# Narrower third slot group and five VectorE steps handed to ScalarE in a four-layer graph network

## The chip, the cores and the metric

The kernel runs on one core of one Trainium2 chip, as one launch. The metric is the device time of that launch in microseconds (us), the median of three runs. Names used below: PE is TensorE (PEld its weight loads), DVE is VectorE, ACT is ScalarE, POOL is GpSimd, SP is SyncE, which here issues the DMAs.

## The reference

128 graphs of 64 nodes with 128 features each pass through four residual layers. An entry of `adj` is nonzero for about a quarter of the node pairs; it is both the edge mask and the edge weight. What matters here, cut from the reference:

```python
# layer 0: continuous filter over edges; h = relu(layernorm(x))
g  = exp(coeff * (e[..., None] - offsets)**2)            # 64 offsets per edge
Wf = ssp(g @ W1.T + b1) @ W2.T + b2                      # per edge, 128 wide
y  = einsum('bjf,bijf->bif', h @ Wa.T, Wf * A * A)
x  = x + ssp(y @ Wd1.T + bd1) @ Wd2.T + bd2              # ssp = softplus - ln 2
# layer 1: hyperbolic graph attention (c = 1)
res   = tanh(|mx| / |x| * artanh(|x|)) * mx / |mx|       # mobius_matvec, per node
h     = proj(mobius_add(proj(res), bias))
x_loc = 2 / lambda(h_i) * artanh(|s|) * s / |s|,  s = mobius_add(-h_i, h_j)   # per edge
att   = sigmoid(silu([x_self, x_loc] @ att_w1.T + att_b1) @ att_w2.T)
x     = x + (sum_j att * x_loc * mask -> MLP -> expmap, logmap, silu, expmap)
# layer 2: degree-normalised aggregation, layer 3: mean of messages and update
```

The artanh of a small argument divided by the argument is 1 + z/3 + z^2/5 + ..., z being the square of the argument.

## The kernel before

**Groups and pairs.** The graphs are worked off in 16 groups of 8. Two graphs lie side by side on the 128 partitions, so a group is 4 pairs (`NP`). Tiles named "dense" are 128 by 4 by 64, that is 256 columns: one entry per pair of nodes. Tiles named "tiny" are 128 by 4: one scalar per node. "Wide" tiles are 128 by 4 by 128.

**Slots.** The edge stages (`layer0`, `layer1_edges`) don't work on 64 by 64 dense entries. `order` sorts the nodes of each graph by degree, and each node gets slots for its neighbours: 8 in the first part, 8 more in the second, and a third part gives further slots to the nodes of the highest degrees alone. `BLOCKS` tells the three parts: in an entry `(k, r0, n, k0)`, `n` nodes from rank `r0` on get `k` slots each, for the neighbours from number `k0` on. The first two parts are one block and 512 columns wide, the third is six blocks and 264 columns. `spread` (a coefficient on each slot), `gather` (the sum over a node's slots) and the building of the one-hot tile `oh` at the end of `order` issue one DVE instruction per block. The other edge steps (filter matmuls on PE, exponentials, logarithms, Silu and Tanh on ACT, products on DVE) issue instructions as wide as the part. In the profile's shapes a form of 264 or 528 (twice 264) columns belongs to the third part, one of 512 or 1024 to the first two. At the very end `enough` compares every node's degree with what `BLOCKS` holds, by `STEPS`; where it doesn't suffice, a branch runs `dense_stack`, the same network over all 64 by 64 entries, after the slot version.

**Order of the work.** The program is straight-line code. `Weave` decides, when the program is built, in which order the steps of all stages are put on the engines: each stage is a generator that yields an engine whenever it goes on to another one, and the weave takes the step that can start first by the estimated durations in `about`; among steps about as early, the one with the lowest key. The key is the stage's due time (`2 * g` and an offset by stage) plus an entry of the table `LATE`, which lists corrections step by step. On the chip each engine then works off its own list in that order, and semaphores hold it where an input isn't ready. The functions Exp and Ln need one ACT table and Silu and Tanh another; the outer loop sets where the table is changed, four times a group.

**The steps that the change touches.**

- `layer1_nodes`, start: PE multiplies layer 0's sums by `wd1T` into a PSUM bank (`sm`); DVE adds the bias `bd1` into `spn` (tile `a0`, in the profile `a<-sm,c_L_gnn_bd`); DVE limits it, ACT takes Exp and Ln.
- `layer1_nodes`, node scalars: `s` is the limited norm; ACT takes two logarithms (`at_p`, `at_m`); DVE forms the artanh quotient `r`, then `z = s * s`, and `series` replaces `r` where `z` is small by a polynomial in `z` (tiles `at_z`, `at_m`).
- `layer1_nodes`, dense coefficients: the same with the dense tiles `rt` (the quotient), `e3` (shown as `e`) and `rs` (the polynomial).
- `layer1_nodes`, end: the dense coefficient `pq` (in tile `rs`) is split into three bf16 parts `pqs`: cast, subtract, cast, subtract, all on DVE.
- `layer1_edges`, `rows`: PE spreads `pqs` to the slots by `oh`; `rest1` and `rest2` are the node-wise end of layer 1 and layers 2 and 3 of an earlier group, woven between.

Of the kernel before, what the change touches and what calls it, by code (L numbers as in the profile page):

```python
# [11 lines left out]
F32 = mybir.dt.float32  # L12
U32 = mybir.dt.uint32
I32 = mybir.dt.int32
AF = mybir.ActivationFunctionType
ALU = mybir.AluOpType
AX = mybir.AxisListType

B, N, D = 128, 64, 128
NG = 64  # L20
NP = 4
GROUPS = B // (2 * NP)
P = 128
# [24 lines left out]
def dense_stack(ctx: ExitStack, tc: tile.TileContext, ins, out: bass.AP):  # L48
# [691 lines left out]
    with tc.manual_schedule(engines={mybir.EngineType.Activation}):  # L740
# [3 lines left out]
        for g in range(GROUPS):  # L744
# [11 lines left out]


BLOCKS = [[(8, 0, 64, 0)], [(8, 0, 64, 8)],
          [(20, 0, 1, 16), (13, 1, 4, 16), (8, 5, 8, 16), (6, 13, 7, 16), (4, 20, 15, 16),
           (2, 35, 13, 16)]]  # L760
WIDTHS = [sum(k * n for k, _, n, _ in c) for c in BLOCKS]
OFFS = [sum(WIDTHS[:i]) for i in range(len(WIDTHS))]
SLOTS = sum(WIDTHS)
RC = max(r + n for _, r, n, _ in BLOCKS[2])
STEPS = [(48, 2.0), (35, 2.0), (20, 2.0), (13, 2.0), (5, 5.0), (1, 7.0)]
SOFT_MAX = 40.0
LN2_HALF = float(0.5 * np.log(2.0))
ROOT_HALF = float(np.sqrt(0.5))
M_MAX = 40.0
# [2 lines left out]
PE, DVE, ACT, POOL = "PE", "DVE", "ACT", "POOL"  # L772
# [12 lines left out]
def about(engine, op, args, kw):  # L785
# [14 lines left out]
    if engine == ACT:  # L800
# [5 lines left out]


LATE = {
    "attention": (0, -0.5),
    "coefs_of": (1.25, 0.75, -2.25),  # L810
    "coefs_of2": (2.75,),
    "duo": (2.5, 3.5),
    "duo2": (0, 2.5, -2),
    "filter_of": (0.75, 3, -0.25, -2.25, -2, -2.75),
    "filter_of2": (-2.75, 1.75, 2.5, 1.75, -2.5),
    "layer1_nodes": (0, -0.25, 0, 0, 0, 0, 0, 3, -3.5, 0, 0, 0, -0.5, -5.5, 0, 2.25, -1.75, 0, 0, 0,
        0, 0, 0, -2.5, 0, 0, 0, 0, 0, -1.25, 0, 0, 0, 2, 0, 0.75, 0, 0, 0, 0, 0, 0, 0, 0, 0.5),
    "neighbours": (-0.25, -3.5),
    "neighbours2": (1.25,),
    "normed_x": (0, 0, 0, 0, 0, 0, 1.5),  # L820
    "one_minus_z": (3.75,),
    "order": (-0.25, -2.75, 2.25, 0, 0, -5, 0, -3.75, 0, 1.75, -6.75, -3, 3.5, 0, 0, -2.75, -2.75,
        3.25, 1.75, 0.5),
    "rest1": (-3, 0, 0, -3, 0, 0, 0, -3.5, -1.75, 0, 0, 0, 0, 0, -1.75, 0, 0, 0, 3.75),
    "rest2": (2.25, 4.5, 0, 0, 0, 0, 0, 0, 0, 0, 0, -4, 0, -3.75, 0, 1.25, 0, 0, 0, 0, -3, 0, -2.25,
        0, -3.5, 0, 0, 1.25, 3),
    "rows": (0, -1.25),
    "rows2": (2.5,),
    "scores_of": (-1.25, -1.5, -3.5, -1.5),
    "scores_of2": (0, -3.25, 0, -3.5),  # L830
    "slots_ranks": (3.5, 0, 4.75),
    "squares": (2.25, 9.5),
    "squares2": (0, 2.75),
    "turned_from": (3.5,),
    "weights_of": (-3,),
    "weights_of2": (0, -2.5, -2.25),
}


# [30 lines left out]
def on(engine, *takes, after=(), table=None):  # L870

    return engine, takes, after, table
# [98 lines left out]
def sparse_stack(ctx: ExitStack, tc: tile.TileContext, ins, out: bass.AP, flag):  # L971
# [3 lines left out]
    const = ctx.enter_context(tc.tile_pool(name="s_const", bufs=1))  # L975
    pers = ctx.enter_context(tc.tile_pool(name="s_pers", bufs=2))
    wide = ctx.enter_context(tc.tile_pool(name="s_wide", bufs=1))
    edge = ctx.enter_context(tc.tile_pool(name="s_edge", bufs=2))
    dense = ctx.enter_context(tc.tile_pool(name="s_dense", bufs=1))
# [4 lines left out]
    w = Weave()  # L984
    V, S, G, T = (Timed(e, name, w) for e, name in ((nc.vector, DVE), (nc.scalar, ACT),
                                                    (nc.gpsimd, POOL), (nc.tensor, PE)))
    BF, U16 = mybir.dt.bfloat16, mybir.dt.uint16

    def bl(ap, n):

        return ap.unsqueeze(len(ap.shape)).to_broadcast([*ap.shape, n])
# [19 lines left out]
    for e in (0.5, -0.5, -0.25):  # L1011
        exps[e] = const.tile([P, 2 * NP], F32, name=f"exp{len(exps)}")
        G.memset(exps[e], e)

    gi = const.tile([P, 1], I32, name="gi")
    G.iota(gi[0:NG, :], [[0, 1]], base=0, channel_multiplier=1)
# [34 lines left out]
    def column(name):  # L1051
        t = const.tile([P, 1], F32, name="c_" + name)
        nc.sync.dma_start(out=t, in_=ins[name].rearrange("(d o) -> d o", o=1))
        return t
# [31 lines left out]
    b1, bd1, b2s = (column("L0_gnn_" + n) for n in ("b1", "bd1", "b2"))  # L1086
# [130 lines left out]
    def wtile(name, bufs=None):  # L1217
        return wide.tile([P, NP, D], F32, name=name, tag=name, **({"bufs": bufs} if bufs else {}))

    def etile(name, bufs=1):  # L1220
        return dense.tile([P, NP, N], F32, name=name, tag=name, bufs=bufs)

    def ttile(name, *shape, bufs=1):
        return tiny.tile([P, *(shape or (NP,))], F32, name=name, tag=name, bufs=bufs)

    def flat(t):
        return t.rearrange("q p n -> q (p n)")
# [10 lines left out]
    act = S.activation  # L1238
# [30 lines left out]
    def reduce_d(dst, src):  # L1269
        V.tensor_reduce(dst, src, AX.X, ALU.add)  # L1270
# [36 lines left out]
    def normed(dst, x, mv, r):  # L1307

        V.tensor_tensor(dst, x, bl(mv[:, :, 0], D), ALU.subtract)
        V.scalar_tensor_tensor(dst, dst, 0.0, bl(r, D), ALU.max, ALU.mult)  # L1310

    def series(r, z, mask, poly):

        V.tensor_scalar(poly, z, 1.0 / 7, None, ALU.mult)
        for c in (1.0 / 5, 1.0 / 3):
            V.scalar_tensor_tensor(poly, poly, c, z, ALU.add, ALU.mult)
        V.tensor_scalar(poly, poly, 1.0, None, ALU.add)
        V.tensor_scalar(mask, z, 0.01, None, ALU.is_lt)
        V.copy_predicated(r, mask.bitcast(U32), poly)

    def root(dst, src, e):
# [4 lines left out]
    def artanh_over(r, s, hn):  # L1326
# [6 lines left out]
        V.tensor_scalar(E.bitcast(I32), E.bitcast(I32), 0x7F800000, None, ALU.bitwise_and)  # L1333
        V.tensor_scalar(ef, E.bitcast(I32), -float(127 << 23), LN2_HALF / (1 << 23),
                        ALU.add, ALU.mult)
# [38 lines left out]

    def slot_tile(name, c, prs, bufs=2):
        W, n = WIDTHS[c], prs.stop - prs.start
        t = edge.tile([P, NP * WIDTHS[2]], F32, name=name, tag=name, bufs=bufs)
        return t[:, 0:n * W].rearrange("q (p w) -> q p w", w=W)

    def prior(*keys):  # L1380
# [112 lines left out]
    def enough():  # L1493
# [3 lines left out]
        V.tensor_scalar(cap, deg, -16.0, None, ALU.add)  # L1497
        for r, more in STEPS:
            V.tensor_scalar(step, place, float(r), more, ALU.is_lt, ALU.mult)
# [154 lines left out]
    def layer1_nodes(g, st):  # L1654
# [4 lines left out]
        spn, ex = wtile("a0"), wtile("a1")  # L1659
        pt = bank()  # L1660
        pre = flat(pt)
# [2 lines left out]
        T.matmul(pre.rearrange("q (x r) -> q x r", r=N)[:, :, 0:RC], lhsT=wd1T, rhs=ys[2],  # L1664
                 start=False, stop=True)
        w.release("ys", st["ys_used"])
        yield on(DVE)
        V.tensor_scalar(flat(spn), pre, bd1, None, ALU.add)
        w.release("sm")
        V.tensor_scalar(ex, spn, SOFT_MAX, None, ALU.min)  # L1670
        w.event("soft_ready", g)
        yield on(ACT, table="log")
# [62 lines left out]
        s, r = ttile("s"), ttile("r")  # L1735
        V.tensor_scalar(s, xn, ATMAX, None, ALU.min)
        yield on(ACT, table="log")
        lp, lm = ttile("at_p"), ttile("at_m")
        act(lp, s, AF.Ln, bias=1.0, scale=1.0)
        act(lm, s, AF.Ln, bias=1.0, scale=-1.0)  # L1740
        yield on(DVE)
        z, rs, mask = ttile("at_z"), ttile("at_r"), ttile("at_k")
        V.tensor_tensor(lp, lp, lm, ALU.subtract)
        V.reciprocal(rs, s)
        V.scalar_tensor_tensor(r, lp, 0.5, rs, ALU.mult, ALU.mult)
        V.tensor_tensor(z, s, s, ALU.mult)
        series(r, z, mask, lm)
        arg = ttile("arg")
        V.tensor_tensor(arg, r, s, ALU.mult)
        V.tensor_tensor(arg, arg, rr[:, 0], ALU.mult)  # L1750
# [2 lines left out]
        te, t, tq = (ttile(f"th{k}") for k in range(3))  # L1753
# [93 lines left out]
        e1, e2, e3, e4, bR = (etile(n) for n in ("e1", "e2", "e3", "e4", "bR"))  # L1847
# [9 lines left out]
        rt, rs, mask = etile("rt"), etile("rs"), etile("mask")  # L1857
# [18 lines left out]
        V.tensor_scalar(rt, rt, ATMAX, None, ALU.min)  # L1876
        yield on(ACT, table="log")
        act(rt, rt, AF.Ln, bias=1.0)
        yield on(DVE, after=[("e4", g)])
        w.event("nodes_log", g)  # L1880
        V.scalar_tensor_tensor(rt, e4, -0.5, rt, ALU.mult, ALU.add)
        V.tensor_tensor(rt, rt, rs, ALU.mult)
        yield on(DVE)
        series(rt, e3, mask, rs)
        yield on(DVE)
        V.tensor_tensor(rt, rt, e2, ALU.mult)
        qd = dense.tile([P, NP, 2, N], F32, name="qd", tag="qd", bufs=2)
        qn, dc, mp, pq = qd[:, :, 0, :], qd[:, :, 1, :], etile("mp", 2), rs
# [6 lines left out]
        cs = ttile("cs", bufs=2)  # L1895
        reduce_d(cs, dc)

        yield on(DVE, after=[("U", g)])
        pqs = dense.tile([P, 3, NP, N], BF, name="pqs", tag="pqs")
        V.tensor_copy(pqs[:, 0], pq)  # L1900
        V.tensor_tensor(e4, pq, pqs[:, 0], ALU.subtract)
        V.tensor_copy(pqs[:, 1], e4)
        V.tensor_tensor(pqs[:, 2], e4, pqs[:, 1], ALU.subtract)

        yield on(DVE)
        Sx, S3 = st["Sx"], [wide.tile([P, NP, P], BF, name=f"Sx{k}", tag=f"Sx{k}") for k in range(3)]
        scaled(Sx, Sx, cs)
        for k in range(2):
# [360 lines left out]
def gnn_stack_kernel(tc: tile.TileContext, ins, out: bass.AP):  # L2269
    nc = tc.nc  # L2270
    with tc.tile_pool(name="flags", bufs=1) as flags:
        flag = flags.tile([P, 1], I32, name="flag")
        sparse_stack(tc, ins, out, flag)
        short = nc.values_load(flag[0:1, 0:1], min_val=0, max_val=P)
        with tc.If(short > 0):
            dense_stack(tc, ins, out)
# [26 lines left out]
```

## Time and profile before

| what | value |
|---|---|
| median of three runs | 2122.32 us (2122.26 to 2126.36) |
| the profiled execution: time, span | 2121.52 us, 2119.6 us |
| busy: PE, DVE, ACT, POOL | 1806.3, 1847.9, 1641.1, 364.5 us |
| mean granted TensorE clock | 0.94 |
| table loads on ACT | 64, 1283 ns each |
| DMA | 13.94 MB, 7 GB/s on average |

Busy time is the time in which an engine had an instruction in work. The profile names groups of instructions by the tile they write and the tiles they read, with the buffer numbers left out, then shape and type, count, total busy time and the mean duration of one. All instructions carry line 853, since a helper (`Timed`) issues them; so the tile names tell the steps apart. Durations of neighbouring DVE or ACT instructions overlap by some 0.07 to 0.1 us, so the distance from start to start is a little shorter than a duration where the second doesn't need the first's result, and a little longer where it does.

### The profile page before, as it was taken

What the parts mean: (1) busy time and instruction counts of PE and PEld (TensorE: products, weight loads), DVE (VectorE), ACT (ScalarE), POOL (GpSimd) and SP (SyncE); (2) the same over time, 40 slices, a digit from 0 to 9 for tenths busy, and PEclk for the clock granted to TensorE, in tenths of its full rate; (3) what the DMA queues carried; (4) which work ended last, traced back from release to release, by engine and by line L of the source; (5) the groups of instructions that cost most, each with busy time, mean ns of one, the idle gap of its engine ahead of it and who ended that gap; (6) DMA issues with size and microseconds to landing.
All of it is one profiled execution on the core that took longest, in us unless ns stands there. A gap on an engine that the chain in (4) does not pass through costs nothing.

```text
span 2119.6 us, 31941 instructions
## 1 busy us (share of the span) xinstructions
PE 1806.3 (85%) x11223; PEld 866.0 (41%) x11223; DVE 1847.9 (87%) x4828; ACT 1641.1 (77%) x3364; POOL 364.5 (17%) x362
## 2 busy tenths in 40 slices
PE   4869897998989898998989889898989889896773
PEld 2333343444444344444444444444434444443342
DVE  5669789999999999999999999999999999897742
ACT  3767887979698887979798897969888796975531
POOL 1011012021212203021221202121220302111121
PEclk9979999999999999999999999999999999997765
DMA  2000000000000000000000000000000000000000
GB/s 55 3 6 1 1 6 1 6 8 6 1 8 6 8 6 8 6 8 6 1 8 6 9 6 9 6 1 8 6 9 1 9 1 6 1 1 6 6 5 8
DMA packets 29531, 13.94 MB, mean 7 GB/s; under 512 B 10544, under 2 KB 29360, under 8 KB 29360
## 3 DMA queue, kind: packets, MB, share of 16 engines
q1 hardware_dynamic: 29360, 11.80, 2.1%
q8 instruction: 90, 1.47, 0.3%
q14 instruction: 81, 0.66, 0.1%
HBM read 7.61 MB, written 4.19 MB: 6 GB/s over the span
## 4 chain that ended last, share of the span: by engine, by line
PE 37%; DVE 36%; ACT 19%; issue 7%; POOL 0%; SPq 0%; DMA 0%; DVEq 0%; ACTq 0%; POOLq 0%
PE big L853 25%; PE sm L853 9%; ACT ex L853 6%; DVE va L853 5%; DVE ex L853 4%; PE sl L853 4%; ACT e L853 4%; DVE th L853 4%; DVE y L853 2%; ACT ra L853 2%; DVE ah L853 2%; DVE v L853 2%; ACT n L853 2%; DVE att L853 2%; DVE oh L853 1%
## 5 line engine op out<-in xcount | busy, mean ns | idle before, releaser
L853 PE MATMUL big<-ex,w2T 128*128 128x512 f32 (+1 forms) x768 | 320.2, 542 | 41.8 <-ACT ex L853 20.6
L853 ACT ACTIVATE ex<-big,c_L_gnn_att_b 128x1024 f32<-128x1024 f32 (+1 forms) x192 | 185.5, 974 | 105.0 <-PE big L853 103.2
L853 PE MATMUL big<-e,w1T 64*128 64x512 f32 (+1 forms) x768 | 201.5, 624 | 68.0 <-ACT e L853 47.8
L853 ACT ACTIVATE ex<-big,c_L_gnn_b 128x1024 f32<-128x1024 f32 (+1 forms) x192 | 185.7, 976 | 44.1 <-PE big L853 44.0
L853 PEld LDWEIGHTS big<-ex,w2T 128*128 128x128 f32 x768 | 131.7, 189 | 198.6 <-ACT ex L853 69.5
L853 PE MATMUL big<-va,U 64*128 64x512 f32 (+1 forms) x768 | 186.5, 563 | 29.1 <-DVE va L853 26.8
L853 PE MATMUL big<-va,a 64*128 64x512 f32 (+1 forms) x768 | 181.1, 568 | 10.7 <-DVE k_s L853 3.8
L853 PE MATMUL sl<-ex,aw2b 128*64 128x512 f32 (+1 forms) x768 | 180.7, 549 | 5.5 <-ACT th L853 4.3
L853 DVE SCALAR_TENSOR_TENSOR ex<-big,c_L_gnn_b,ra 128x1024 f32<-128x1024 f32 x128 | 163.7, 1279 | 16.0 <-PE big L853 15.6
L853 ACT ACTIVATE ex<-ex 128x1024 f32<-128x1024 f32 (+1 forms) x192 | 173.9, 925 | 0.2
L853 ACT ACTIVATE ra<-big 128x528 f32<-128x528 f32 (+1 forms) x192 | 166.3, 886 | 8.1 <-PE big L853 7.6
L853 DVE TENSOR_REDUCE y<-ex 128x128 f32<-128x1024 f32 x128 | 155.3, 1213 | 0.6
L853 ACT ACTIVATE th<-sl,hab 128x512 f32<-128x512 f32 (+1 forms) x192 | 118.1, 615 | 45.4 <-PE sl L853 45.4
L853 PE MATMUL big<-slot_r,Sx 64*128 64x512 bf16 (+1 forms) x1152 | 138.9, 346 | 0.0
L853 POOL TENSOR_TENSOR k_r<-k_r,exp 128x4 f32<-128x4 f32 x32 | 32.4, 1013 | 583.1 <-DVE k_r L853 578.7
L853 PEld LDWEIGHTS big<-e,w1T 64*128 64x128 f32 x768 | 68.9, 204 | 155.6 <-ACT e L853 55.1
L853 ACT ACTIVATE va<-va,sr 128x512 f32<-128x512 f32 (+1 forms) x192 | 123.1, 650 | 3.1 <-DVE va L853 2.9
L853 PE MATMUL big<-oh,pqs 64*64 64x512 bf16 (+1 forms) x1152 | 123.3, 348 | 0.0
L853 DVE COPY_PREDICATED va<-slot_r,big 128x1024 f32<-128x1024 uint16 (+1 forms) x96 | 106.5, 1111 | 9.7 <-PE big L853 9.7
L853 DVE SCALAR_TENSOR_TENSOR th<-th,oh 128x1024 f32<-128x1024 f32 (+1 forms) x80 | 99.2, 1240 | 13.8 <-ACT th L853 13.8
L853 ACT ACTIVATE e<-e 128x1024 f32<-128x1024 f32 (+2 forms) x144 | 106.7, 752 | 1.1
L853 PE MATMUL big<-va,ones 64*64 64x512 f32 (+1 forms) x768 | 97.4, 559 | 11.0 <-DVE va L853 11.0
(479 smaller groups left out, 3832.4 us busy)
## 6 DMA issues: line engine op xcount, KB each, us to landing
x<-in_x_dram SPq DMA_DIRECT2D x16, 256.0 KB, 2.9
out_dram<-v SPq DMA_DIRECT2D x16, 256.0 KB, 2.3
adj<-in_adj_dram SPq DMA_DIRECT2D x16, 128.0 KB, 2.3
rt<-in_L_gnn_att_w_dram SPq DMA_DIRECT2D x2, 64.0 KB, 1.9
rs<-in_L_gnn_mlp_w_dram SPq DMA_DIRECT2D x2, 64.0 KB, 2.0
wupd<-in_L_gnn_W_upd_dram SPq DMA_DIRECT2D x1, 128.0 KB, 3.6
w<-in_L_gnn_W_msg_dram SPq DMA_DIRECT2D x2, 64.0 KB, 3.3
r_L_gnn_bd<-in_L_gnn_bd_dram SPq DMA_DIRECT2D x1, 64.0 KB, 3.1
```

What stands on the lines that cost most here:

```text
L853: return f(*args, **kw)
```

## The change

The third part becomes five blocks with 242 columns in all (`STEPS` follows). The bias `bd1` is added by an ACT Identity. The two casts of `pqs` become ACT Copies. The polynomial of the small arguments becomes a square with a constant: 0.2 z^2 + z/3 + 1 = (A z + B)^2 + (1 - B^2), with the square on ACT, in a tile of its own (`poly` for the dense, `at_r` for the tiny one), and the constant added on DVE; the bound below which it is used goes from 0.01 to 0.006. The tiny `z` itself becomes an ACT Square. The table `LATE` has new entries, so the order of the instructions on every engine is another one. The slot tiles shrink from 1056 to 1024 columns.

```diff
 BLOCKS = [[(8, 0, 64, 0)], [(8, 0, 64, 8)],
-          [(20, 0, 1, 16), (13, 1, 4, 16), (8, 5, 8, 16), (6, 13, 7, 16), (4, 20, 15, 16),
-           (2, 35, 13, 16)]]
+          [(18, 0, 2, 16), (11, 2, 4, 16), (7, 6, 6, 16), (5, 12, 18, 16), (2, 30, 15, 16)]]
...
-STEPS = [(48, 2.0), (35, 2.0), (20, 2.0), (13, 2.0), (5, 5.0), (1, 7.0)]
+STEPS = [(45, 2.0), (30, 3.0), (12, 2.0), (6, 4.0), (2, 7.0)]
+SERIES_A = float(np.sqrt(0.2))
+SERIES_B = 1.0 / (6.0 * SERIES_A)
+SERIES_REST = 1.0 - SERIES_B * SERIES_B
...
 LATE = {
-    "attention": (0, -0.5),
-    "coefs_of": (1.25, 0.75, -2.25),
+    "attention": (0, 0, 0, 1),
+    "coefs_of": (1,),
...
+    series_b = const.tile([P, 1], F32, name="series_b")
+    G.memset(series_b, SERIES_B)
...
+    def series_square(poly, z):
+        act(poly, z, AF.Square, scale=SERIES_A, bias=series_b)
+
     def series(r, z, mask, poly):
-        V.tensor_scalar(poly, z, 1.0 / 7, None, ALU.mult)
-        for c in (1.0 / 5, 1.0 / 3):
-            V.scalar_tensor_tensor(poly, poly, c, z, ALU.add, ALU.mult)
-        V.tensor_scalar(poly, poly, 1.0, None, ALU.add)
-        V.tensor_scalar(mask, z, 0.01, None, ALU.is_lt)
+        V.tensor_scalar(poly, poly, SERIES_REST, None, ALU.add)
+        V.tensor_scalar(mask, z, 0.006, None, ALU.is_lt)
         V.copy_predicated(r, mask.bitcast(U32), poly)
...
-        t = edge.tile([P, NP * WIDTHS[2]], F32, name=name, tag=name, bufs=bufs)
+        t = edge.tile([P, max(2 * WIDTHS[0], NP * WIDTHS[2])], F32, name=name, tag=name, bufs=bufs)
...
-        yield on(DVE)
-        V.tensor_scalar(flat(spn), pre, bd1, None, ALU.add)
+        yield on(ACT)
+        act(flat(spn), pre, AF.Identity, bias=bd1)
         w.release("sm")
+        yield on(DVE)
         V.tensor_scalar(ex, spn, SOFT_MAX, None, ALU.min)
...
         act(lm, s, AF.Ln, bias=1.0, scale=-1.0)
+        act(z, s, AF.Square)
+        series_square(rs, z)
         yield on(DVE)
-        z, rs, mask = ttile("at_z"), ttile("at_r"), ttile("at_k")
         V.tensor_tensor(lp, lp, lm, ALU.subtract)
-        V.reciprocal(rs, s)
-        V.scalar_tensor_tensor(r, lp, 0.5, rs, ALU.mult, ALU.mult)
-        V.tensor_tensor(z, s, s, ALU.mult)
-        series(r, z, mask, lm)
+        V.reciprocal(lm, s)
+        V.scalar_tensor_tensor(r, lp, 0.5, lm, ALU.mult, ALU.mult)
+        series(r, z, mask, rs)
...
         act(rt, rt, AF.Ln, bias=1.0)
+        poly = etile("poly")
+        series_square(poly, e3)
         yield on(DVE, after=[("e4", g)])
...
-        series(rt, e3, mask, rs)
+        series(rt, e3, mask, poly)
...
+        pqs = dense.tile([P, 3, NP, N], BF, name="pqs", tag="pqs")
+        for k in range(2):
+            yield on(ACT)
+            act(pqs[:, k], (pq, e4)[k], AF.Copy)
+            yield on(DVE)
+            V.tensor_tensor((e4, pqs[:, 2])[k], (pq, e4)[k], pqs[:, k], ALU.subtract)
+
         yield on(DVE, after=[("U", g)])
-        pqs = dense.tile([P, 3, NP, N], BF, name="pqs", tag="pqs")
-        V.tensor_copy(pqs[:, 0], pq)
-        V.tensor_tensor(e4, pq, pqs[:, 0], ALU.subtract)
-        V.tensor_copy(pqs[:, 1], e4)
-        V.tensor_tensor(pqs[:, 2], e4, pqs[:, 1], ALU.subtract)
-
-        yield on(DVE)
```

## The prediction

> **What bounds the kernel now.** I read the page's busy rows and slices first, then busy time by equal stretches, then the groups by shape, the DVE timeline of one group of graphs, and last the chain of waits.
>
> ```profile
> PE 1806.3 (85%) x11223; PEld 866.0 (41%) x11223; DVE 1847.9 (87%) x4828; ACT 1641.1 (77%) x3364; POOL 364.5 (17%) x362
> DVE  5669789999999999999999999999999999897742
> PE 37%; DVE 36%; ACT 19%; issue 7%; POOL 0%; SPq 0%; DMA 0%; DVEq 0%; ACTq 0%; POOLq 0%
> ```
>
> DVE is the busiest engine, and its slices stand at 9 from about 400 to 1850 us; only the start and the end are thinner. The last line, the chain that ended last, is split between PE, DVE and ACT, as it must be where three engines are nearly full. The stretches tell more:
>
> ```profile
> core 0: us, PE busy (x) PEld busy (x) DVE busy (x) ACT busy (x) POOL busy (x), PEclk, DMA share, GB/s
> 845.70:966.90 121.20, 109.05 (x700) 51.71 (x698) 114.39 (x297) 102.03 (x211) 22.59 (x22) 0.98 0.02 7
> 966.90:1088.00 121.10, 108.69 (x702) 51.95 (x704) 114.67 (x300) 102.53 (x211) 23.18 (x22) 0.98 0.02 6
> ```
>
> In the middle one group of graphs takes 121.2 us, again and again with the same pattern. DVE is busy for 114.6 of them (95%), PE for 108.9 (90%), ACT for 102.3 (84%). DVE's waits for other engines add up to about 3.2 us a group there; the rest of its 6.6 idle us are the small gaps between dependent instructions. So DVE is the bound, and work that leaves it should shorten the period nearly one to one until PE's 109 us are reached. In the last 170 us (1950 on) DVE is busy for half the time only: there the chain of one group sets the pace.
>
> **The change part by part, per group.** Rows (mean ns, all by shape) and timeline pieces:
>
> ```profile
> L853 DVE TENSOR_SCALAR a<-sm,c_L_gnn_bd 128x512 f32<-128x512 f32 x16 | 11.9, 744 | 5.3 <-PE sm L853 5.3
> L853 DVE CAST pqs<-rs 128x256 bf16<-128x256 f32 x16 | 4.5, 284 | 0.0
> L853 ACT ACTIVATE w<-sm,c_L_gnn_mlp_b 128x512 f32<-128x512 f32 x16 | 11.0, 688 | 16.4 <-PE sm L853 16.4
> L853 ACT ACTIVATE Sx<-n 128x512 bf16<-128x512 f32 x32 | 20.0, 625 | 3.2 <-DVE n L853 3.2
> L853 ACT ACTIVATE rt<-rt 128x256 f32<-128x256 f32 x48 | 19.9, 414 | 0.9 <-DVE rt L853 0.3
> ```
>
> ```profile
> 763.51 0.29 DVE L853 TENSOR_SCALAR rs<-e 128x256 f32<-128x256 f32 x1
> 763.84 0.88 DVE L853 SCALAR_TENSOR_TENSOR rs<-rs,e 128x256 f32<-128x256 f32 x2
> 764.76 0.29 DVE L853 TENSOR_SCALAR rs<-rs 128x256 f32<-128x256 f32 x1
> ```
>
> *Off DVE by moving.* I count from start to start, since most of these are dependent. The dense polynomial loses its first three instructions: 763.51 to 764.76, 1.25 us; the added constant stays. The tiny one loses the square and three steps: 729.71 to 730.50, 0.79 us. `bd1`: 701.51 to 702.30, 0.79. The casts: 769.99 to 770.31 and 770.77 to 771.10, 0.65. Together 3.48 us.
>
> *Off DVE by 22 columns and one block.* Six sets of blocks are worked per group: building `oh`, two spreads, two gathers in layer 0, one in layer 1. Rows of 80 and 256 elements (`y<-two`, 234 and 411 ns) give 1.0 ns an element; six of them take 1.54 us in the timeline where their durations add up to 1.97, so one costs about 0.07 us beyond its elements. 88 elements and one instruction fewer: 0.16 us, six times 0.94. The four products `two` save 44 elements at 1.04 ns (1279 ns at 1024, 762 at 528): 0.18. Two predicated copies at 1.10 ns: 0.10. The product `th` with 88 fewer: 0.09. Together 1.31 us. DVE in all: 4.8 us a group, 77 us in 16.
>
> *Onto ACT.* The Identity lies between 596 ns (`a<-sm`, Relu without a bias tile) and 688 (the row above): 0.64. A 256-column cast is nearest to the 414 ns of `rt<-rt` (half of the `Sx` cast's 625 would be 0.31): two, 0.82. The dense square 0.41 to 0.51 (a bias tile adds 95 ns between `ra<-big`, 1023, and `e<-big,noff`, 1118): 0.46. Two tiny squares at 195 to 290 ns: 0.45. Sum 2.4 us. The third part gives back 1056 elements at 0.82 ns (`ra`: 1023 ns at 1024, 611 at 528): 0.87. Net +1.5 us a group: ACT goes to 104 us, still behind DVE. Identity, Copy and Square need no table of their own: Copy and Square already stand on both sides of the table loads, and the changed program loads tables as often as before.
>
> *Off PE.* Per instruction (busy divided by count) the w2T matmul goes from 0.489 us at 512 columns to 0.273 at 264, and likewise for the other seven kinds; 22 columns fewer save 4.9 (w2T), 3.4 (w1T), 2.6 (`va,a`), 2.6 (U), 2.4 (aw2b), 1.9 and 1.9 (the bf16 ones) and 1.4 us (ones) over the run: 21 us, 1.3 a group. PE goes to 107.6.
>
> *A rule against the change.* The rows say that a cast costs 0.28 to 0.29 us on DVE and about 0.41 on ACT, so engine time is lost. The Trainium skill, page "ScalarE: Activation LUTs", section "Rules for kernel authors", says the same as advice: adds and multiplies belong on VectorE, not on ScalarE. By that rule the two casts would lose 2 x 0.12 us a group, 4 us in all; by my sum they win 0.65 us a group, 10 in all, because the engine they leave is the one that the others wait for. The case's own stretches (95% against 84%) decide for the second.
>
> *New waits.* Each moved step makes a hop DVE to ACT and back, and ACT's queue is in order: a step can stand behind a 1024-wide activation (0.93 to 1.1 us). Covers, by the order in which the changed program's instructions stand on DVE: between the end of `pq` and the first subtraction there are two dense steps and five gathers (about 2.2 us); between the subtraction and the second, two products and a dense step (2.3 us); between `s` and the `at_p` difference, three dense steps and the reduction `mhb` (1.9 us). Before `rt<-e,rt` there is none: it waits for the logarithm of `e4`, which stands behind the new dense square, a known wait of 0.54 us now, perhaps 1 us after. For `bd1` the limiting `a<-a` is held by the Identity, and behind it on DVE stand two 1024-wide spreads which the next layer 0 starts from; four 128-wide products (1.1 us) stand in front of it.
>
> *The new order.* It also moves POOL's work against DVE's. This costs DVE time already:
>
> ```profile
> 796.48 2.52 POOL L853 TENSOR_TENSOR a<-xp,o_mv 128x512 f32<-128x512 f32 x1
> 798.02 1.00 DVE L853 TENSOR_TENSOR rb<-rb,un 128x4 f32<-128x4 f32 x1
> 799.08 3.34 POOL L853 TENSOR_TENSOR xp<-xp,r_L_gnn_bd 128x512 f32<-128x512 f32 x1
> 801.21 1.22 DVE L853 TENSOR_TENSOR k__7224<-k__7224,ur 128x4 f32<-128x4 f32 x1
> ```
>
> A 128x4 DVE product that elsewhere takes 0.16 us ends here just as POOL's 512-wide one ends. With `s` (1.24), the small `att` sum (1.07 for 0.34) and one `th` (0.71) such stalls come to about 4.3 us a group. POOL has the same work after the change, and the same kinds of small DVE steps lie next to it; I take this as even, with 1.5 us a group either way. At the start SP issues the weights in another sequence: layer 1's first matrix, for which PE waits until 11.66 us, now stands 12th instead of 17th, at 0.47 us each, and layer 0's stand later by as much: even, within 2 us.
>
> **Sum.** If all 4.8 us come through in every group, 77 us. Lower end: each engine's part counts only by the share of its busy time that lies on the chain: DVE 763 of 1848 us (41%), PE 43%, ACT 25%: 77 x 0.41 + 21 x 0.43 - 24 x 0.25 = 35 us. The steady rows lie nearer the first. I take 3.8 of 4.8 us (1 us for the uncovered wait and for PE and ACT now at 92 and 88% of a shorter period) in the 11 groups from 520 to 1850 us, 42 us, and for five groups' work at both ends two fifths of 24 us, 10. So 52 us off the execution's 2121.5 (span 2119.6 and 1.9 around it): 2069.5, and as that lies 0.8 below the median, 2070.
>
> **Rivals.**
> 1. PE and ACT take over. DVE keeps its saving, but the period is then held by PE's chain through ACT: the waits of PE for `e` (5.6 us a group) and of ACT for `big` (9 us) stay, as the chain shares say. 35 us or less: 2087 to 2105. For it: 37% of the chain is PE. Against it: DVE at 95% with 3.2 us of waits.
> 2. Slower: the hops are not covered. Five hops a group (Identity, the scalar squares, the dense square, two casts) at one 1024-wide activation each, 1.1 us, make 5.5 us against 4.8 won: 0.7 x 16 = 11 us, 2133. It decides from 0.96 us of uncovered wait per hop on. Against it: the covers above, 1.1 to 2.3 us but for the one.
> 3. The change doesn't do what it says: five blocks don't hold every node, and the branch runs the dense stack too. The adjacency that the reference draws has at most 30 neighbours, and by rank no node exceeds 16 plus its third-part slots, though with nothing to spare at five ranks. If it did: 4096 instead of 1288 columns a pair, an estimate of 6700 us more.
>
> **How the numbers follow.** My forecast (2040 to 2085) 0.62, rival 1 0.22, rival 2 0.12, rival 3 0.01; 0.03 for a change within 0.2% (4 us, about what a measurement of this kernel can tell from no change). Low end: all 77 us and 0.5 us a group of stalls gone, 2037. High end: rival 1's 2105 and a little of the rest, 2110; past it lies little more than rival 2. Faster 0.84 (the first two), same 0.03, slower 0.13.
>
> **What would show it.** Right: DVE busy near 1775 us, PE near 1785, ACT near 1665, POOL unchanged, 64 table loads; a period of 116.5 to 118 us; the products `two` near 716 ns and `ra` near 575 at 484 columns. Wrong: a period of 119 us or more with DVE's idle share grown (rivals 1 and 2, told apart by whether PE's busy share or DVE's waits for ACT grew), new long 128x4 DVE steps (POOL), or a second program behind the first (rival 3).

## The result and the profile after

The changed kernel is slower, by 1.7%: 2158.12 us (2156.07 to 2160.16, four executions) against 2122.29 us (2120.2 to 2126.36, four) of the kernel before on the same chip, a ratio of 1.0166 (95% interval 1.0148 to 1.0185). The profiled execution took 2160.16 us, its span 2158.2. The forecast of 2070 us missed by 88 us, and its range did not hold the time.

From the page of the changed kernel, the busy row, the DVE slices, the granted clock and the shares of the chain:

```profile
PE 1829.9 (85%) x11223; PEld 883.3 (41%) x11223; DVE 1800.8 (83%) x4568; ACT 1656.7 (77%) x3460; POOL 330.7 (15%) x362
DVE  5668788888989898898989899898888889787742
PEclk9979999998999999998999999999999989898675
PE 49%; DVE 25%; ACT 21%; issue 4%; POOL 0%; DMA 0%; SPq 0%; DVEq 0%; ACTq 0%; POOLq 0%
```

DVE did lose work (47 us busy), yet its slices now alternate between 8 and 9, and its share of the chain fell from 36 to 25%. PE has less to do than before and is busy for 23.6 us more, since its clock is at half more often ("Off PE, and the clock" below). Two periods, from one `hh<-n,sc` on DVE to the next, in the windows view (busy time of PE, its weight loads, DVE, ACT and POOL, then the granted clock):

```profile
1006.90:1132.66 125.76, 111.91 (x700) 53.13 (x700) 111.75 (x281) 103.22 (x217) 20.16 (x21) 0.95 0.02 6
1132.66:1257.13 124.47, 111.45 (x700) 53.37 (x700) 111.65 (x282) 103.13 (x217) 20.18 (x21) 0.95 0.02 6
```

A period is 124.2 us on average (the eleven from 511 us on) where 117.4 were forecast. No engine is above 90% of it.

### The profile page after: what moved, and what is told of

The parts are those of the page before. It is cut to its first block, busy times and chain, and to the rows that moved or that the text cites. A ratio compares the mean times of both kernels' runs of the same rounds, so it can differ in the third digit from the quotient of the medians.

```text
span 2158.2 us, 31801 instructions
## 1 busy us (share of the span) xinstructions
PE 1829.9 (85%) x11223; PEld 883.3 (41%) x11223; DVE 1800.8 (83%) x4568; ACT 1656.7 (77%) x3460; POOL 330.7 (15%) x362
## 4 chain that ended last, share of the span: by engine, by line
PE 49%; DVE 25%; ACT 21%; issue 4%; POOL 0%; DMA 0%; SPq 0%; DVEq 0%; ACTq 0%; POOLq 0%
PE big L858 32%; PE sm L858 13%; ACT ex L858 6%; DVE va L858 4%; DVE att L858 3%; PE sl L858 3%; DVE oh L858 2%; ACT e L858 2%; ACT L858 2%; ACT va L858 2%; DVE th L858 2%; DVE y L858 2%; ACT ra L858 2%; ACT th L858 1%; ACT v L858 1%
## 5 line engine op out<-in xcount | busy, mean ns | idle before, releaser
L858 PE MATMUL big<-ex,w2T 128*128 128x512 f32 (+1 forms) x768 | 328.9, 554 | 13.4 <-ACT ex L858 11.1
L858 PE MATMUL big<-e,w1T 64*128 64x512 f32 (+1 forms) x768 | 207.5, 634 | 78.8 <-ACT e L858 74.0
L858 PEld LDWEIGHTS big<-ex,w2T 128*128 128x128 f32 x768 | 137.9, 196 | 166.4 <-issue 85.0
L858 ACT ACTIVATE ra<-big 128x484 f32<-128x484 f32 (+1 forms) x192 | 167.3, 875 | 47.8 <-PE big L858 46.5
L858 PE MATMUL big<-va,a 64*128 64x512 f32 (+1 forms) x768 | 192.9, 587 | 2.0 <-ACT e L858 1.1
L858 POOL TENSOR_TENSOR k_r<-k_r,exp 128x4 f32<-128x4 f32 x32 | 38.7, 1210 | 877.3 <-DVE k_r L858 877.3
L858 ACT ACTIVATE th<-sl,hab 128x512 f32<-128x512 f32 (+1 forms) x192 | 118.4, 617 | 23.1 <-PE sl L858 21.7
L858 DVE TENSOR_TENSOR va<-oh,adjT 128x1024 f32<-128x1024 bf16 (+1 forms) x144 | 105.7, 753 | 23.6 <-PE big L858 21.4
L858 ACT ACTIVATE va<-va,sr 128x512 f32<-128x512 f32 (+1 forms) x192 | 119.9, 647 | 4.0 <-DVE va L858 4.0
L858 DVE TENSOR_TENSOR va<-oh,qd 128x1024 f32<-128x1024 bf16 (+1 forms) x144 | 112.0, 779 | 2.2
```

The lines of the kernel that those rows point to most:

```text
L858: return f(*args, **kw)
```

## Experiments

Every ratio is taken against the kernel before, measured again beside each set of kernels: 2122.3 us for sections 1 and 2, 2123.2 for section 3, 2121.3 and 2124.2 for the two halves of section 4, 2121.0 for section 5. So medians of different sets can be off against each other by some 3 us. One source makes all kernels. The planner is told the durations and steps of one version (old or new order), and the instructions of the other may be issued in their place. So order and work can be exchanged:

```diff
-        V.tensor_tensor(z, s, s, ALU.mult)          # the planner notes its duration
+        as_dve(NP)                                  # the duration alone
+        if not W_POLY:
+            nc.vector.tensor_tensor(z, s, s, ALU.mult)   # the work alone
...
-LATE = {...}
+LATE = OLD_LATE if not PLAN_NEW else NEW_LATE
```

### 1. The work and the order apart

> All of the change's work (five blocks, 242 columns, the five steps on ACT) with the instructions of every engine in the order of the kernel before: the planner is given the old costs, the old steps and the old LATE table, only the issued instructions are the new ones. Theory 1 (the work is worth what was forecast, the new order loses it by leaving PE without work at the Silu-to-logarithm table change, so that its clock falls): 2045 to 2090 us, period 116.5 to 119 us, about 5 us of half clock a period as before. Theory 2 (the DVE-ACT-DVE hops of the moved steps eat the saving, in whatever order): 2130 to 2165 us, DVE waits for ACT on rt, pqs and a grown by 5 us a group.

Measured: 2134.62 us, ratio 1.0025 (0.9991 to 1.0059). Its ten executions lie on two levels, three at 2113 us (mean granted clock 0.943) and seven at 2134 to 2138 (0.926); the profile is one of the latter. The figure lies within theory 2's range, the lower level in neither.

> The reverse: the work of the kernel before (six blocks, 264 columns, bias, casts and polynomial on DVE) in the new order. Theory 1: no better than the changed kernel, 2158 to 2235 us (2158 plus at most the 77 us of work put back), with about 17 us of half clock a period. Theory 2: without the hops the new order does no harm, 2085 to 2130 us.

Measured: 2187.95 us, ratio 1.0303 (1.0286 to 1.0320), in theory 1's range.

So neither theory stands alone. The new order costs 65.6 us with the old work and 23.5 with the new. The old order alone does not bring the forecast gain either. Within the new order the change's work gains 29.8 us (2187.95 to 2158.12), within the old order it loses 12.3 at the median (and gains 9 at the lower level): what the work is worth depends on the order.

### 2. Keeping PE at work, in the wrong place

In the new order PE stops for 4.2 us at the table change (3.05 in the kernel before), waiting for the Exp of `e`. Then it stops a second time for `pos`. PE's timeline of the changed kernel (start, duration, what; in brackets the idle time before and what ended it):

```profile
978.68 1.16 PE L858 MATMUL sm<-wlinT,n 128*128 128x128 f32 x8
984.05 2.08 PE L858 MATMUL big<-e,w1T 64*128 64x512 f32 x4 [4.21 <-ACT e L858]
986.06 0.40 PE L858 MATMUL sm<-last_d,bones_b 128*128 128x256 bf16 x1
987.54 0.37 PE L858 MATMUL sm<-pos,bones 128*128 128x256 bf16 x1 [1.08 <-DVE pos L858]
```

The four `w1T` matmuls at 984.05 take 2.08 us; the same four at full clock took 1.13 (from 1091.24 on in `old_order_left_out`). Matmuls without use were meant to hold the clock up:

```diff
         evac(mx, pt)
+        for _ in range(3):
+            nc.tensor.matmul(flat(pt), lhsT=ident, rhs=flat(hT), start=True, stop=True)
         w.release("sm")
```

> The changed kernel with three added matmuls of 512 columns per group (128x128, fp32, no use of their result), put on PE in layer1_nodes right after the copy of mx out of its PSUM bank, before the wait for the Exp of e, to keep PE at work over the table change. Theory 1: the clock stays up or returns earlier; of the 5.6 us a period of clock lost beyond the kernel before some 2 to 5 us come back, 2095 to 2140 us, although PE has 1.8 us a group more to do. Theory 2: nothing gained, 2158 to 2185 us.

Measured: 2177.12 us, ratio 1.0258 (1.0217 to 1.0299).

> The kernel before with the same three added matmuls per group. It loses 3 us of clock a period at the same place. Theory 1: between 2085 and 2125 us (DVE is its bound, so less comes back). Theory 2: 2122 to 2150 us, the added work costs or is hidden.

Measured: 2151.86 us, ratio 1.0135 (1.0118 to 1.0152).

Both are slower, the first within theory 2's range, the second just above it. In the second the clock hardly fell between 500 and 1850 us (13.7 us at half clock where the kernel before has 64.9), but the matmuls held the PSUM bank `sm`. From the waits of DVE (total us, times, longest):

```profile
DVE dn L900 <- PE sm L900: 34.8, 14, 3.5
```

In the kernel before, the same wait adds up to 1.2 us. The place was wrong, so this pair decides little.

### 3. The work left out, and parts of the change

```diff
+            nc.vector.tensor_scalar(flat(ex), pre, bd1, SOFT_MAX, ALU.add, ALU.min)   # bias and limit in one
...
+        D_.tensor_scalar(poly, z, SERIES_REST, None, ALU.add)                         # no polynomial
...
+                V.tensor_tensor((pqs[:, 0], pqs[:, 2])[k], pq, (e4, pqs[:, 0])[k], ALU.subtract)  # no casts
```

> Order of the kernel before, five blocks, and the five steps taken off DVE without being put on ACT: the bias and the limit are one DVE instruction (and the maximum is taken of the softplus alone), the polynomial is only its added constant, the two casts are left out (the second bf16 part is read from the first). So DVE and PE have what the changed kernel has, ACT has no new step and no hop. Theory H (in the old order the hops to ACT and back eat the saving: DVE waited 30 us for the Identity and 20 us for the casts): 2055 to 2090 us, period 117 to 119 us. Theory P (PE's chain through ACT at the table change takes over as soon as DVE has less to do): 2105 to 2125 us, period 120 to 121.5 us, with hops or without.

Measured: 2107.83 us, ratio 0.9925 (0.9899 to 0.9952). Theory P.

> The same leaving out in the new order. Theory H: hops are placed well in the new order, so little changes, 2140 to 2158 us. Theory P: the same, 2140 to 2158 us, since PE is the bound there. If it falls below 2115 us, the hops are what is wrong with the new order too.

Measured: 2159.45 us, ratio 1.0183 (1.0153 to 1.0213). Just above both ranges, and the same as with the steps on ACT (2158.1): in the new order neither the hops nor ACT's time cost anything.

> Order of the kernel before with five blocks and the polynomial as a square on ACT; the bias and the casts stay on DVE. These two parts wait for nothing new by much. Theory H: 2075 to 2100 us (3.3 of the 4.8 us a group). Theory P: 2105 to 2125 us.

Measured: 2130.16 us, ratio 1.0040 (1.0027 to 1.0053). Above both ranges.

> Order of the kernel before with its six blocks and its polynomial; only the bias and the two casts go to ACT. Theory H: they lose about 3.1 us of waits a group for 1.44 us won, 2135 to 2155 us. Theory P: DVE is relieved a little and waits a little, 2115 to 2130 us.

Measured: 2131.12 us, ratio 1.0044 (1.0028 to 1.0061). Between the theories.

The first of these is the central run. DVE and PE have less to do by all that the change takes from them, ACT has nothing new, nobody hops, the order is the old one, and only about 15 of the forecast 77 us appear. Its pairs of periods last 242.35 us (121.67 and 120.68), as those of the kernel before do (120.84 and 121.51); the gain lies outside them. DVE's busy time fell by 40.7 us there (1847.9 to 1807.2), less than the 77 counted: 11.5 us of the difference are a collision with POOL that section 5 shows, the rest is not assigned.

### 4. Keeping PE at work in the right place

The added matmuls now go into the bank that the first `w1T` matmul after the table change overwrites, directly before it:

```diff
             pre = big()
+            for _ in range(w.warm):
+                nc.tensor.matmul(pre[:, 0, 0:512], lhsT=ident, rhs=bm(ident, NP), start=True, stop=True)
+            w.warm = 0
             for b, rows in enumerate(side):
```

> The kernel before with six added matmuls (128x128, 512 columns, fp32, their result is overwritten) per group on PE, right before the first w1T matmul after the table change, in the same PSUM bank; PE sits idle there for 3 to 4 us, so they delay little. Theory L (PE's stop at the table change halves its clock, the clock comes back only on a fixed grid of 3.41 us, and so the group's period is held at a multiple of half a grid step: 71 steps for two groups before and with five steps left out, 36 for one with the change's work in the old order): no dips at the switch, a period off the grid, 2090 to 2118 us. Theory P (the chain PE-ACT-DVE through the table change sets the period whatever the clock): 2115 to 2135 us.

Measured: 2139.16 us, ratio 1.0077 (1.0055 to 1.0100).

> All of the change's work in the order of the kernel before, with the same six added matmuls per group. Theory L: the 4.8 us a group that DVE was relieved of show at last, 2060 to 2100 us. Theory P: 2110 to 2140 us, as without them.

Measured: 2131.87 us, ratio 1.0048 (1.0030 to 1.0067).

> The same with the five steps left out and not put on ACT (as before: bias and limit in one DVE instruction, constant polynomial, no casts). Theory L: 2050 to 2090 us. Theory P: 2100 to 2115 us.

Measured: 2121.23 us, ratio 0.9995 (0.9983 to 1.0007).

> The changed kernel with eight added matmuls per group right before the first w1T matmul after the table change (PE is idle for 4.2 us there). Theory L: the dips at the change go, the later breaks of this order (the wait for pos, and that for e and v some 25 us on) may keep one of them: 2110 to 2145 us. Theory P: 2150 to 2175 us.

Measured: 2163.42 us, ratio 1.0195 (1.0166 to 1.0224).

All four lie above theory L's ranges. The dose was wrong. From PE's timeline of `old_order_left_out_warm` (each added matmul is two records):

```profile
1089.70 5.42 PE L1680 MATMUL big<-ident 128*128 128x512 f32 x12
1095.04 1.99 PE L900 MATMUL big<-e,w1T 64*128 64x512 f32 x8
```

The Exp of `e` started at 1091.71 and took 1.0 us; PE came 2.3 us late. The four runs were repeated with three added matmuls, and four in the new order.

> As with six added matmuls, but three: an added one took 0.90 us (six: 5.42 us), so six overran the Exp that PE waits for by 2.3 us a group, and three (2.7 us) end just before it. Theory L (with the clock kept up the period leaves the grid): 2139 less 2.3 x 16 = 2102 us, range 2095 to 2115. Theory P (the chain, not the clock, holds the period): 2119 to 2126 us.

Measured: 2108.55 us, ratio 0.9923 (0.9906 to 0.9939). Theory L's range, and the fastest of the kernels that leave nothing out.

> The change's work in the order of the kernel before with three added matmuls a group. Theory L: 2132 less 37 = 2095 us, range 2085 to 2108. Theory P: 2110 to 2138 us as without them.

Measured: 2120.44 us, ratio 0.9981 (0.9966 to 0.9996). Theory P's range.

> Five steps left out, three added matmuls a group. Theory L: 2121 less 37 = 2084 us, range 2075 to 2098. Theory P: 2103 to 2113 us.

Measured: 2099.43 us, ratio 0.9879 (0.9863 to 0.9896). Between the two ranges.

> The changed kernel with four added matmuls a group (3.6 us in 4.2 us of idle time). Theory L: 2163 less 3 x 16 = 2115 us, range 2105 to 2135, less if the later breaks of this order keep a dip. Theory P: 2150 to 2165 us.

Measured: 2159.85 us, ratio 1.0165 (1.0148 to 1.0182). Theory P's range.

With the old work in the old order the time at half clock between 500 and 1850 us falls from 64.9 to 10.2 us. Over the three kernels of the old order 8 to 16 us are won against the median of the same kernel without the added matmuls; but the lower level of `old_order_new_work` (2113) is 7 us below its kernel with them. Up to 9 of the 16 are not the clock's: with the shift, 48 small `th` steps of DVE take 164 ns instead of 349 (POOL). Theory L in its strong form falls: with the clock up, the common period is 119.9 us with the old work and 120.0 with 4.8 us less counted for DVE, and the whole kernel is 9.1 us shorter. In the new order nothing is won; the waits of PE show why (after first, then `new_order_warm4`):

```profile
PE big L858 <- ACT e L858: 75.1, 33, 4.2
PE sm L858 <- DVE pos L858: 12.7, 13, 1.1
```

```profile
PE big L900 <- ACT e L900: 26.9, 30, 1.3
PE sm L900 <- DVE pos L900: 24.5, 13, 2.2
```

The waits for `e` shrink by 48 us, mostly filled with the added matmuls, and 12 us of that turn into a longer wait for `pos`, which stands behind them in PE's list.

### 5. ACT's time without the hops, and the blocks alone

> The old order with the five steps left out, plus three ACT instructions of 256 columns a group (a square and two copies) at the places where the dense polynomial's square and the two casts of the change stand on ACT; they read a tile that has long been ready, and nobody reads their result. So ACT's time for them is there, the hops are not. Theory A (ACT is the bound in this stage: busy 14.6 of 14.7 us there before, and its time for the three, 1.1 us a group, is added to the chain): 2108 plus 18 = 2126 us, range 2119 to 2134. Theory W (the waits from engine to engine, not ACT's time, cost the 27 us between the left-out kernel and that with the steps on ACT): 2105 to 2113 us.

```diff
+            nc.scalar.activation(idle, e3, AF.Square, scale=SERIES_A, bias=series_b)   # where the square stands
...
+                    nc.scalar.activation(idle, e3, AF.Copy)                            # where each cast stands
```

Measured: 2129.57 us, ratio 1.0037 (1.0025 to 1.0049). Theory A: of the 26.8 us between the left-out kernel and the median of that with the steps on ACT, 21.7 come without any hop, from ACT's time for the three dense steps (1.1 us a group in the chain, 18 us; the other 4 are not assigned). The clock moves along with it: the time at half clock between 500 and 1850 us goes from 75.1 to 112.6 us, so the run does not part ACT's time from what the longer waits do to the clock. The kernels with the stop filled do: both have 10.2 us at half clock, and the new ACT steps with their hops still cost 21.0 us (2099.4 to 2120.4). The price is not the same in every course of the clock: the lower level of `old_order_new_work` lies only 5 us above the left-out kernel, and no trace of it was kept.

> The part of the change that gives work to nobody else: five blocks of 242 columns, all five steps on DVE as before, the old order, and three added matmuls a group at the table change. ACT and PE both get shorter by 0.9 and 1.3 us a group. Theory A: between old_order_warm3 (2108.5) and old_order_left_out_warm3 (2099.4), since the steps on DVE cost little: 2096 to 2108 us, 0.7 to 1.2% below the kernel before. Theory P in its strict form (a chain of PE and ACT alone): 2099 us.

Measured: 2130.56 us, ratio 1.0047 (1.0029 to 1.0066). A miss: 22.0 us above the same kernel with six blocks. Two groups of DVE carry it (of `old_order_warm3`, then of this kernel; count, total and mean ns):

```profile
L900 DVE SCALAR_TENSOR_TENSOR th<-th,oh 128x1056 f32<-128x1056 f32 x16 | 20.0, 1252 | 8.5 <-ACT th L900 8.5
L900 DVE COPY_PREDICATED th<-at_k,th 128x4 f32<-128x4 uint32 x16 | 2.7, 166 | 0.6
```

```profile
L900 DVE SCALAR_TENSOR_TENSOR th<-th,oh 128x968 f32<-128x968 f32 x16 | 31.5, 1970 | 8.1 <-ACT th L900 8.1
L900 DVE COPY_PREDICATED th<-at_k,th 128x4 f32<-128x4 uint32 x16 | 12.7, 792 | 0.5
```

The narrower product takes 0.72 us longer than the wider one, and a 128x4 copy 0.63 longer: 21.5 us in 16 groups. The product's cause is in the timelines; the copy's is not shown. First `old_order_warm3`, then this kernel, DVE and POOL of each (start, duration):

```profile
1201.90 1.25 DVE L900 SCALAR_TENSOR_TENSOR th<-th,oh 128x1056 f32<-128x1056 f32 x1
1202.15 2.12 POOL L900 TENSOR_TENSOR n<-n,r_L_gnn_b_lin 128x512 f32<-128x512 f32 x1 [8.53 <-ACT n L900]
```

```profile
1208.85 2.23 DVE L900 SCALAR_TENSOR_TENSOR th<-th,oh 128x968 f32<-128x968 f32 x1
1208.66 1.40 POOL L900 TENSOR_TENSOR n<-n,r_L_gnn_b_lin 128x512 f32<-128x512 f32 x1 [8.25 <-ACT n L900]
```

Whichever starts first about keeps its length (1.25 us; POOL's 1.40 against 1.27 undisturbed), and the other is stretched. The Trainium skill, page "SBUF — State Buffer", section "Who interferes with whom", calls it an exclusive lock on the port pair that the two engines share; these rows agree. With fewer columns DVE comes 0.2 us after POOL instead of 0.25 before it. The 1.97 us stand in the other five-block kernels of the old order too, the longer copy in this one alone; in the new order the product takes 1.21 us.

With the filled kernels of section 4 this run splits the old order's result in another way: five blocks alone cost 22.0 us (2108.6 to 2130.6), the five steps taken off DVE then give 31.1 back (to 2099.4) of the 56 counted for them, and the steps on ACT cost 21.0 (to 2120.4). Here DVE's time seems to count: the blocks' loss is about as large as the 21.5 us of stretches, and 10 of the 31.1 us correspond to the copy's stretch, which the left-out kernel lacks. So the small gain of the left-out kernel is a sum of a loss and a larger gain.

## Why the prediction was wrong

The runs make a ladder from 2122.3 to 2158.1 us (medians of different sets, so each rung is good to some 3 us): 14.5 down for less DVE and PE work with nothing put on ACT (2107.8); 21.7 up for ACT's time for the dense square and the two casts (2129.6); 5.1 up for the rest, namely the hops, the Identity and the tiny squares (2134.6); 23.5 up for the new order (2158.1). Counted by the lower of the two levels of `old_order_new_work` (2113) the last two rungs would be 16 down and 45 up, so the third rung has no firm sign; the first two don't depend on it.

**What bounds the kernel: this step failed.** "DVE is the bound, and work that leaves it should shorten the period nearly one to one" was read from a whole period (95%). The left-out run tests just that, and one fifth came; with the stop filled it was 9 us. Of the steps without the blocks more than half came (31.1 of 56 us), and the blocks' part had the wrong sign (see "Off DVE"). For the dense steps the stage was there to be read in the profile of before. In the 15 us in which the dense polynomial lies:

```profile
996.30:1011.00 14.70, 13.53 (x106) 7.21 (x105) 12.66 (x33) 14.60 (x28) 0.00 (x0) 1.00 0.07 20
```

ACT is busy for 14.60 of 14.70 us, PE for 13.53, DVE for 12.66. The chain of before is ACT, piece after piece, from 996.29 to 1010.86:

```profile
996.29 0.37 ACT U L853
...
1009.86 0.95 ACT ex L853
1010.82 0.04 issue
1010.86 1.98 PE big L853 x4
```

The casts follow about a microsecond behind. DVE's 95% is real, but in this stage DVE has room, so its relief is worth little here and each new ACT instruction lengthens the chain. Why the relief outside this stage (`bd1`, the small polynomial, the blocks) left the common period at 120 us is not separated by a run. In `old_order_new_work` the chain that ended last runs through them:

```profile
1011.57 0.40 ACT poly L1375
1011.97 0.95 ACT e L900
...
1021.62 0.31 ACT pqs L2018
...
1021.96 0.44 DVE e L900
...
1022.42 0.42 ACT pqs L2018
```

**Onto ACT: right in size, wrong in place.** The rows after: `poly` 495 ns, the casts 435 each, the Identity 687, `ra` at 484 columns 577 (forecast 575), `two` 718 (716); ACT's busy time rose by 15.6 us to 1656.7 (forecast 1665). What failed was to price them at nothing because "ACT goes to 104 us, still behind DVE". The lower end of the sum (35 us) took ACT's time at its share of the chain, 25%, and was too mild for the same reason: in this stage of the old order the share is all of it. In the new order ACT's time was as good as free (2159.5 left out, 2158.1 with it), so this step explains the old order's loss and not the last rung. The rule of the Trainium skill (page "ScalarE: Activation LUTs", section "Rules for kernel authors") that adds and multiplies belong on DVE was weighed at 4 us of loss for the casts against 10 of gain. In the old order the rule's sign was right: the bias and the casts on ACT made the kernel 7.9 us slower (`old_order_bias_casts`); no run has the casts alone.

**New waits.** Five uncovered hops were rival 2's reason, at 88 us in all. All the rest of ACT's new work together with the hops made 5.1 us in the old order by the ladder (16 us less than nothing by the lower level), and nothing in the new one. Its number (2133) is near 2134.6 by chance; its mechanism is not borne out.

**The new order was taken as even: the second failure.** It costs 23.5 us with the new work (45 by the lower level), the largest rung. The term was argued from POOL's collisions alone, whose sum did stay about even: by the rows, `s`, `rb`, the `k` product and the small `th` gave back 45 us, while `nn`, `d_ca` and the two `att` sums took 40 more. But they moved to a worse place. DVE and POOL of the changed kernel after the table change:

```profile
982.70 2.38 DVE L858 TENSOR_TENSOR att<-att,att 128x256 f32<-128x256 f32 x2
985.00 1.24 DVE L858 TENSOR_SCALAR nn<-n 128x8 f32<-128x8 f32 x1
987.07 0.42 DVE L858 TENSOR_TENSOR pos<-ident,degs 128x256 bf16<-128x256 f32 x1
```

```profile
982.43 1.27 POOL L858 TENSOR_TENSOR x<-x,r_L_gnn_b 128x512 f32<-128x512 f32 x1
983.66 1.22 POOL L858 TENSOR_TENSOR w<-hh,cs 128x512 f32<-128x512 f32 x1
984.96 1.26 POOL L858 TENSOR_TENSOR w<-w,r_L_gnn_mlp_b 128x512 f32<-128x512 f32 x1
```

The small `nn` (0.16 us before) ends just as POOL's last product does, and `pos`, for which PE waits until 987.54, comes after three short steps more. That this chain holds the new order is read from these rows and from the longer wait for `pos` in `new_order_warm4`; no run took POOL's work away there, so it is argued, not shown. Shown is that in this order the moved steps (left out: 2159.5) and PE's stop at the table change (filled: 2159.9) are not what holds it. What gives the new order's further 42 us with the old work stays open.

**Off DVE.** DVE was forecast at 1775 us and has 1800.8. The moved instructions are gone from its rows. The term for the 22 columns and the block (1.31 us a group, 21 us won) had the wrong sign in the old order with the stop filled: 22.0 us lost, with 21.5 us of stretches on DVE. In the other five-block kernels of the old order the narrower `th` alone took back 11.5 us by its collision; had these counted in full, the left-out run would have shown 26 us, a third of the 77. That is not tested, and in the new order this collision is hardly there.

**Off PE, and the clock.** PE was forecast at 1785 us and has 1829.9. The clock, which the forecast did not weigh, is at half for 116.1 us between 500 and 1850 us (64.9 before). It goes with PE's waits, as the last section shows; filling the stop was worth 8 to 16 us at most in the old order against the medians and nothing in the new.

**Rivals.** Rival 1 had the mechanism of the first rung (PE and ACT take over), but kept DVE's saving and the sign. Rival 3 is out: no second program ran.

## What to carry to other kernels

Before moving work from a full engine to a less full one, look up both engines in the stage where the step runs, not in the period: an engine that is 84% busy overall was 99% busy just there. To price a move, run it first with the work left out and nothing put elsewhere; here this one run would have put the gain in the old order at 15 us. Take its parts singly as well, since a gain and a loss can hide in one sum. An instruction order found for one set of durations is a part of the kernel, so changing it is a change to be priced by itself, and exchanging order and work separately is a cheap way to do so.

## What the runs showed of the hardware

**The clock is set on a grid, by the last window's busy share.** Between 500 and 1850 us every stretch at half clock in the 20 traces lasted 3.41, 6.83 or 10.24 us, and within a trace the edges lie on one grid of 3.413 us, to 0.01 us. The same two stops of PE (0.64 and 1.22 us in `old_order_blocks_poly`, 0.71 and 1.22 in the kernel before) halve the clock in the one and not in the other, since the grid cuts them differently. Windows on the grid (the columns as above), first `old_order_blocks_poly`, then before:

```profile
933.47:936.88 3.41, 1.54 (x9) 0.72 (x9) 3.38 (x6) 1.98 (x8) 1.54 (x2) 1.00 0.00 0
936.88:940.30 3.42, 3.42 (x14) 1.31 (x12) 3.35 (x6) 1.06 (x1) 0.00 (x0) 0.50 0.00 0
```

```profile
1051.72:1055.13 3.41, 2.19 (x16) 1.14 (x18) 3.41 (x4) 0.85 (x2) 1.31 (x1) 1.00 0.02 5
1055.13:1058.55 3.42, 3.42 (x24) 1.11 (x22) 3.38 (x9) 2.82 (x3) 0.00 (x0) 1.00 0.01 2
```

A window with PE busy for 45% is followed by half clock, one with 64% is not. Over all 20 traces (some 8300 windows at full clock from about 390 to 1890 us), each window below 46% was followed by half clock and none above 58%; at half clock each window above 87% brought the full clock back and none below 83% did. The Trainium skill, page "TensorE: Matmul & The Clock Gate", section "What's actually happening", gives a free-running window of 3413 ns, which agrees; it speaks of an idle window, where here half a window of work was too little.

**Periods lock to that grid.** Two groups before last 242.3 us, 71 steps of the grid (242.35); `old_order_new_work`, `old_order_blocks_poly` and `old_order_left_out_act` have 122.88 us, 36 steps, for many groups on end. This fits periods equal to the hundredth; it may also be why one kernel has two levels, but only one of them was traced. It does not explain the lost gain, since without the dips 119.9 and 120.0 us remained.
